# A scan, two quantized feed-forward layers and an attention block on one core: scaled third q, ternary rounding on ACT, norms on DVE, a butterfly on POOL, order planned by phase

## The chip, the cores and the metric

The kernel runs on one core of a Trainium2 chip. The time is the device time of one execution in microseconds (us); the figure of the kernel before is the median of three runs. PE is TensorE (PEld its weight loads), DVE is VectorE, ACT is ScalarE, POOL is GpSimd, SP is the queue that issues the DMAs.

## The reference

Two layers are added onto x, which has 128 sequences of 32 time steps and 256 features:

```python
x = x + L0_ffn(L0_cond(q0=cond, p0=cond, drive=x, coupling, bias), w_gate, w_up, w_down)
x = x + L1_ffn(L1_cond(x, emb=cond, ...), w_gate, w_up, w_down)

# L0_cond: 32 Runge-Kutta steps of coupled oscillators, each of four derivatives
dq = q - q ** 3 / 3.0 - p + drive + tanh(q) @ coupling.T + bias
dp = EPSILON * (q + ALPHA - BETA * p)        # after each step q and p are clipped to +-20
# L0_ffn: silu(gate) * up, inputs and weights rounded in blocks of 32 with a shared exponent
# L1_cond: rms norm, scale and shift from cond; q, k, v; per head, with 16 features,
q = rms_norm(q, g_q); k = rms_norm(k, g_k)   # then softmax(q k^T / 4) v, and o + o @ W_out
# L1_ffn: a Hadamard transform of the input ahead of each product, 8 bit rounding of it,
q = clip(round(w / mean(abs(w))), -1, 1) * mean(abs(w))   # ternary weights; silu(gate) * up
```

## The kernel before, in words

All work is one list of items. `Work.add` notes for each its engine, a cost in us, the buffers that it reads and writes, and a rank (its place in the program). Some 30 pools of tiles serve the buffers (`slim` 128x256, `mid` 128x512, `wide` 128x1024, `tiny` 128x32; PSUM banks `ps_stage`, `ps_sum`, `ps_turn`, `ps_gu` in phase one, four `ps_one` and two double `ps_two` in phase two). `Work.run` is a list scheduler: it places the items on five engines in the order in which they can start, by their costs, gaps between engines (`TAIL`, `HOP`, `WITHIN`) and free tiles. `Work.order` runs it 40 times forth and back over all items, taking the ends of one pass as the priorities of the next, and keeps the order that ends first. The engines then issue in that order, each its own queue, so an instruction whose input is late holds all that are behind it on its engine. `emit` (L1345) writes all items of phase one (rank below 100) before those of phase two. `keep_warm` puts products of zeros where the plan has gaps on PE (L1354).

Phase one has the scan and the first feed-forward layer. `step` (L577 on) is one scan step over 128 rows x 256 features. For each of the four derivatives a PSUM bank `ps[i]` gathers a linear part written by DVE (`nest`, one scalar_tensor_tensor, L552), the drive d times a scaled identity (`plus`, L587), tanh times the coupling matrix (`slope`, L594 and L601), and earlier slopes times a scaled identity. The cubes are a Square on ACT (L595) times q on POOL (L608). Sums w and z for the end of the step are kept in PSUM by more nests; at its end a DVE operation adds and clips q (L645) and another clips z, the scaled p (L653). `ffn0(t, q)` takes each step's result through the first layer: block maxima and scales on DVE (L688, L666, L678, L671), products with POOL (L914, L956, L964), clipping (L888), transposes by DMA (L434), gate and up on PE (L929), Silu (L937), down (L976), and at last the rms norm of the sum and its transposed copy into `xnT` (L1017), which all of phase two reads. Weights are prepared meanwhile: `mx_weight` for the first layer, and `ternary_weight` for the second, whose loads wait for scan step 24. That one takes the mean magnitude with Abs on ACT (L763), and then per half of a matrix compares on DVE with -0.5 of the mean (L791) and with 0.5 of it (L796).

Phase two, `tokens(g)`, takes 32 tiles of 128 tokens each. Products with `w_qkv` give q and k (L1125, bank `pqk`) and v (L1132, bank `pv`, half of it used). ACT squares q and k (L1142), DVE sums each head (L1143), and `rsqrt` finds the reciprocal root: an affine step on POOL (L1088), a first guess from the bits on DVE (L1091), ten small operations on POOL (L1099 to L1109). DVE multiplies q and k by it (L1148, L1155), POOL multiplies q by the gains (L1160), DVE transposes (L1167, L1169), PE makes small products per head (L1177), softmax runs over DVE and ACT (L1192, L1196, L1199), PE multiplies by v (L1207), and after the output product (L1230) the tokens are rounded to 8 bits (`quantum`, L1071 to L1079). Gate and up (L1263), Silu (L1271) and their product (L1278) follow. Then come three butterfly stages over 1024 columns, two instructions each (L1294), on POOL, DVE, POOL in the first 29 tiles and on DVE in the last three; a transpose (L526), a product with a 128-wide Hadamard matrix (L1305), the rounding (L1313, L1317), the down product (L1328) and the sum (L1335).

Of the kernel before, what the change touches and what calls it, by code (L numbers as in the profile page):

```python
# [13 lines left out]
I32 = mybir.dt.int32  # L14
AF = mybir.ActivationFunctionType
# [22 lines left out]
RSQRT = 8.0 / 3.0  # L38
# [61 lines left out]
class Work:  # L100
# [82 lines left out]
    def run(self, forth):  # L183
# [11 lines left out]
        self.issued, self.last, self.gone = [], dict.fromkeys(ready), set()  # L195
        for item in self.items:
            item.open = len(item.after if forth else item.before)
            item.ready = 0.0
            for b in item.bufs:
                b.left, b.end = 0, 0.0  # L200
                if b.slots and not b.fixed:
                    b.slot = None
                for s in b.slots:
                    s.free = 0.0
        pools = {}
        for item in sorted(self.items, key=lambda i: i.prio):
# [5 lines left out]
        for item in self.items:  # L212
            if not item.open:
                ready[item.engine].append(item)
        done = []
        while len(done) < len(self.items):
# [20 lines left out]
            idle = item.engine == PE and t > now[PE] + 0.05  # L237
# [20 lines left out]
            for i in item.before if forth else item.after:  # L258
                i.ready = max(i.ready, item.end + (self.gap(item, i) if forth else self.gap(i, item)))
                i.open -= 1  # L260
                if not i.open:
                    ready[i.engine].append(i)
        return done

    def order(self):

        for item in self.items:
            for a in item.after:
                a.before.append(item)
            for b in item.bufs:  # L270
                b.fixed = b.slot is not None
            item.prio = item.rank
        best = math.inf
        for n in range(self.ROUNDS):
            self.strict = n > 0
            done = self.run(True)
            end = max(item.end for item in done)
            if end < best:
                best, chosen = end, done
                places = [(b, b.slot) for item in done for b in item.bufs]  # L280
                times = [(item, item.start, item.end) for item in done]
                ends = [(b, b.end) for item in done for b in item.bufs]
            for item in self.items:
                item.prio = -item.end
            self.strict = True
            self.run(False)
            for item in self.items:
                item.prio = -item.end
        for b, slot in places:
            b.slot = slot  # L290
        for b, end in ends:
            b.end = end
        for item, start, end in times:
            item.start, item.end = start, end
        self.keep_warm(chosen)
        return chosen
# [26 lines left out]
def kernel(  # L323
# [153 lines left out]

    P2, P3, END, LAST = rk4()
    S = -END[4]
    h = DT  # L480
    K = (1.0 + h / 2, 1.0 - h / 2 * P2[1], 1.0 - h * P3[1])
    EYES = (h / 2 / K[0], h / 2 / K[1], h / K[2], h / 6, LAST[3], -LAST[4] - h / 6)
    C_SCALES = (*EYES[:3], -h / 6)
    CUBES = tuple((c / 3.0) ** 0.5 for c in (h / 2, h / 2, h, h / 6))
# [94 lines left out]
    def step(t, q, p, d):  # L579
# [11 lines left out]
        def slope(i, qi):  # L591

            th, sq = Buf(slim), Buf(slim)
            add(ACT, 0.32, lambda: nc.scalar.activation(th.ap, qi.ap, AF.Tanh), [qi], [th], rank=rank, table="silu")  # L594
            add(ACT, 0.31, lambda: nc.scalar.activation(sq.ap, qi.ap, AF.Square, scale=CUBES[i]), [qi], [sq], rank=rank)  # L595

            def mm():
                for c in range(NC):
                    for m in range(NC):
                        sl = slice(m * P, (m + 1) * P)  # L600
                        nc.tensor.matmul(  # L601
                            ps[i].ap[:, sl], lhsT=coup[i][:, c, sl], rhs=two(th.ap)[:, c, :],
                            start=False, stop=(c == NC - 1 and m == NC - 1),
                        )
# [23 lines left out]
        plus(2, 2, d)  # L628
        nest(w2, w, LAST[1] / LAST[2], q2, rank)
        nest(z, z, END[1] / END[2], q2, rank)  # L630
        nest(q3, ps[1], K[1], cube, rank, SUB)
        plus(2, 2, q3)
# [10 lines left out]
        add(  # L643
            DVE, 0.335,
            lambda: nc.vector._custom_dve(  # L645
                TENSOR_ADD_SAT, out=qn.ap, in0=ps[3].ap, in1=cube.ap, s0=CLAMP, s1=-CLAMP
            ),
            [ps[3], cube], [qn], rank=rank,
        )
        edge = ALPHA / BETA  # L650
        add(
            DVE, 0.335,
            lambda: nc.vector.tensor_scalar(  # L653
                z.ap, z.ap, (-CLAMP - edge) / S, (CLAMP - edge) / S, ALU.min, ALU.max
            ),
            [], [z], rank=rank,
        )
# [96 lines left out]
    def ternary_weight(w, dst, b_dst, n, rank, after):  # L754
        mag, lim = Buf(tiny), Buf(tiny)
# [29 lines left out]
        add(DVE, 0.1, lambda: ts(lim.ap[:, 0:1], ws, 0.5, None, MULT), [], fills=[lim], rank=rank, after=[own])  # L785
        add(DVE, 0.1, lambda: ts(lim.ap[:, 1:2], ws, -0.5, None, MULT), [], fills=[lim], rank=rank, after=[own])

        for part, raw in enumerate(raws):
            low, wq = Buf(wide), Buf(wide_bf)
            add(  # L790
                DVE, 0.65, lambda raw=raw, low=low: ts(low.ap, raw.ap, lim.ap[:, 1:2], None, ALU.is_lt),  # L791
                [raw, lim], [low], rank=rank, port=True,
            )
            add(
                DVE, 1.2,
                lambda raw=raw, low=low, wq=wq: stt(wq.ap, raw.ap, lim.ap[:, 0:1], low.ap, ALU.is_gt, SUB),  # L796
                [raw, lim, low], [wq], rank=rank, port=True,
            )
            turn_weight(wq, dst, b_dst, part, rows, rank)
# [94 lines left out]
    def ffn0(t, q):  # L894
# [101 lines left out]
        add(POOL, 0.72, rsqrt, [], [ms], rank=rank)  # L996
# [52 lines left out]
    for b_c, c_mat in zip(b_coup[:KPADS], coup):  # L1049
        k_pad = c_mat.rearrange("p c n -> p (c n)").rearrange("p (r a d) -> p r a d", a=4, d=D_HEAD)  # L1050
        pads_ready.append(
            add(POOL, 0.6, lambda k_pad=k_pad: nc.gpsimd.memset(k_pad, 0.0), [], [b_c], rank=float(T))
# [31 lines left out]
    def rsqrt(v, y, scale, eps, rank):  # L1084

        t, u = Buf(tiny), Buf(tiny)
        tt, ts = nc.gpsimd.tensor_tensor, nc.gpsimd.tensor_scalar
        add(POOL, 0.24, lambda: ts(v.ap, v.ap, scale, eps, MULT, ADD), [], [v], rank=rank)  # L1088
        add(
            DVE, 0.12,  # L1090
            lambda: nc.vector.tensor_scalar(  # L1091
                y.ap.bitcast(I32), v.ap.bitcast(I32), -0.5, float(0x5F3759DF), MULT, ADD
            ),
            [v], [y], rank=rank,
        )

        def steps():

            tt(t.ap, y.ap, y.ap, MULT)  # L1099
            tt(t.ap, t.ap, v.ap, MULT)  # L1100
            ts(t.ap, t.ap, -0.5, 1.5, MULT, ADD)
            tt(y.ap, y.ap, t.ap, MULT)

            tt(t.ap, y.ap, y.ap, MULT)
            tt(t.ap, t.ap, v.ap, MULT)
            ts(u.ap, t.ap, 1.0, -10.0 / 3.0, MULT, ADD)
            tt(u.ap, u.ap, t.ap, MULT)
            ts(u.ap, u.ap, 1.0, 5.0, MULT, ADD)
            tt(y.ap, y.ap, u.ap, MULT)  # L1109

        add(POOL, 2.4, steps, [v], [t, u, y], rank=rank, port=True)

    def tokens(g):
# [26 lines left out]
        sq_sum, rstd = Buf(tiny), Buf(tiny)  # L1140
        add(ACT, 0.26, lambda: nc.scalar.copy(v_pad.ap[:, :, :D_HEAD], heads(pv.ap[:, :N])), [pv], [v_pad], rank=rank)
        add(ACT, 0.477, lambda: nc.scalar.activation(sq.ap, pqk.ap, AF.Square), [pqk], [sq], rank=rank)  # L1142
        add(DVE, 0.6, lambda: nc.vector.tensor_reduce(sq_sum.ap, heads(sq.ap), AX.X, ADD), [sq], [sq_sum], rank=rank)  # L1143

        rsqrt(sq_sum, rstd, 1.0 / D_HEAD, EPS_RMS, rank)
# [38 lines left out]
        for k in range(0, PAIRS, PAIRS // 2):  # L1184
            add(
                PE, 0.55, lambda k=k: logits(range(k, k + PAIRS // 2)), [qT, kT], fills=[pl], rank=rank,
# [25 lines left out]
        for k in range(0, HEADS, HEADS // 2):  # L1212
            add(
                PE, 0.63, lambda k=k: attend(range(k, k + HEADS // 2)), [exT, v_pad], fills=[po], rank=rank,
# [70 lines left out]
        for s, engine in enumerate((POOL, DVE, POOL) if g < NT - 3 else (DVE, DVE, DVE)):  # L1285
            dst = Buf(wide)
            for e, op in enumerate((ADD, SUB)):
# [8 lines left out]
                add(engine, 0.6 if engine == DVE else 1.228, butterfly, [src], fills=[dst], rank=rank, port=True)  # L1296
# [120 lines left out]
```

## Time and profile before

| what | value |
|---|---|
| median of three runs (range) | 867.91 us (867.62 to 868.57) |
| the profiled execution, its span | 868.0 us, 866.2 us |
| busy: PE, PEld, DVE | 795.1 us (92%), 598.6 us (69%), 732.2 us (85%) |
| busy: ACT, POOL | 494.0 us (57%), 615.9 us (71%) |
| mean clock granted to TensorE | 0.986 |
| last scan state starts (L645) | 398.0 us |
| first product of phase two (L1125), last sum (L1335) | 431.3 us, 862.9 us |

Busy time is the time in which an engine executes. Matmuls are pipelined and their ends are modelled, so PE shown as busy isn't PE at its peak. A group of instructions has its line, engine, operation, tiles, shapes and count, then busy us and mean ns of one, then the engine's idle time just before them and what ended it. A wait is put down to the instruction that came last.

### The profile page before, as it was taken

The numbers are of one execution on the slowest core, as the hardware profiler recorded it, in microseconds if no ns is written. First come the engines' busy times: TensorE is split into PE (matmuls) and PEld (weight loads), VectorE is DVE, ScalarE is ACT, GpSimd is POOL, SyncE is SP. The second block draws the span as 40 slices with busy tenths as digits, with TensorE's granted clock in tenths as the row PEclk, the third lists the DMA queues.
The fourth block names the chain that finished last, engine by engine and source line by source line (L and its number), as shares of the span: only waits on it lengthen the run. The fifth ranks groups of instructions, "written<-read, shape, count | busy, mean of one in ns | idle before, by whom it ended". The sixth has DMA issues, their size and how long they took to land. (4 is left out here: it accounts for less than half of the span.)

```text
span 866.2 us, 26286 instructions
## 1 busy us (share of the span) xinstructions
PE 795.1 (92%) x10506; PEld 598.6 (69%) x10506; DVE 732.2 (85%) x1863; ACT 494.0 (57%) x1009; POOL 615.9 (71%) x955
## 2 busy tenths in 40 slices
PE   7789999999999999997789999999999999899986
PEld 4566778877788788775456667666667676576765
DVE  6889989999989999998677887778878788887694
ACT  3233465655466665754335667666767555776755
POOL 5698898888768888899574776656685676676320
PEclk9999999999999999999799999999999999999999
DMA  7222232313122242435500113221221221221334
GB/s 241 84 38 53 59 82 59 74 49 83 35 65 68 70 134 56 92 67 110 117 2 15 27 39 65 49 49 32 52 50 48 56 48 42 48 43 46 60 68 86
DMA packets 128891, 55.53 MB, mean 64 GB/s; under 512 B 102144, under 2 KB 127616, under 8 KB 128768
## 3 DMA queue, kind: packets, MB, share of 16 engines
q1 hardware_dynamic: 128768, 53.85, 26.9%
q8 instruction: 82, 1.34, 0.6%
q14 instruction: 41, 0.34, 0.1%
HBM read 21.32 MB, written 8.39 MB: 34 GB/s over the span
## 5 line engine op out<-in xcount | busy, mean ns | idle before, releaser
L1294 POOL TENSOR_TENSOR wide<-wide 128x512 f32<-128x512 f32 x116 | 149.1, 1306 | 68.7 <-DVE wide L1278 33.6
L601 PEld LDWEIGHTS ps_stage<-slim,coup 128*128 128x128 f32 x1024 | 129.3, 192 | 18.1 <-ACT slim L594 10.6
L601 PE MATMUL ps_stage<-slim,coup 128*128 128x128 f32 x1024 | 139.4, 279 | 0.6 <-ACT slim L594 0.3
L608 POOL TENSOR_TENSOR slim<-slim,slim 128x256 f32<-128x256 f32 x96 | 72.4, 755 | 27.7 <-ACT slim L595 23.0
L587 PE MATMUL ps_stage<-slim,eye 128*128 128x256 f32 x256 | 76.6, 392 | 8.1 <-DVE slim L552 7.8
L587 PE MATMUL ps_stage<-drives,eye 128*128 128x256 f32 x256 | 79.2, 392 | 3.3 <-DVE ps_stage L552 2.0
L956 POOL TENSOR_TENSOR mid<-mid,tiny 128x512 f32<-128x512 f32 x64 | 66.2, 1047 | 3.7 <-DVE tiny L678 3.2
L964 POOL TENSOR_TENSOR wide_bf<-mid,tiny 128x512 bf16<-128x512 fp8e4 x64 | 66.5, 1050 | 1.4 <-DVE mid L888 1.1
L594 ACT ACTIVATE slim<-slim 128x256 f32<-128x256 f32 x96 | 39.3, 409 | 47.4 <-DVE slim L552 44.6
L1305 PE MATMUL ps_two<-had_ffn,wide 128*128 128x128 f32 x512 | 63.3, 278 | 1.3 <-DVE wide L1278 1.2
L595 ACT ACTIVATE slim<-slim 128x256 f32<-128x256 f32 x96 | 39.2, 408 | 43.1 <-DVE slim L552 43.0
L1305 PEld LDWEIGHTS ps_two<-had_ffn,wide 128*128 128x128 f32 x512 | 59.9, 192 | 5.4 <-ACT wide L1300 1.9
L1125 PE MATMUL ps_one<-w_qkv_sb,xnT 128*128 128x512 f32 x128 | 60.7, 599 | 0.5 <-DVE mid L1196 0.2
L1313 ACT ACTIVATE wide<-ps_two,magic,tiny 128x1024 f32<-128x1024 f32 x32 | 38.5, 1203 | 39.5 <-DVE tiny L1079 28.0
L587 PEld LDWEIGHTS ps_stage<-slim,eye 128*128 128x128 f32 x256 | 42.0, 190 | 24.0 <-DVE slim L552 16.1
L1294 DVE TENSOR_TENSOR wide<-wide 128x512 f32<-128x512 f32 x76 | 53.3, 727 | 5.9 <-POOL wide L1294 5.9
L1278 DVE SCALAR_TENSOR_TENSOR wide<-ps_two,tiny,mid 128x512 f32<-128x512 f32 x64 | 46.4, 737 | 12.0 <-ACT mid L1271 11.3
L1207 PEld LDWEIGHTS ps_one<-v_pad,mid 32*32 32x32 f32 x4096 | 42.2, 106 | 20.8 <-issue 15.4
L1271 ACT ACTIVATE mid<-ps_two,tiny 128x512 f32<-128x512 f32 x64 | 43.0, 686 | 21.9 <-PE ps_two L1263 21.6
L1207 PE MATMUL ps_one<-v_pad,mid 32*32 32x17 f32 x4096 | 48.0, 181 | 4.5 <-issue 3.0
L587 PEld LDWEIGHTS ps_stage<-drives,eye 128*128 128x128 f32 x256 | 40.3, 193 | 12.3 <-DVE ps_stage L552 7.7
L1263 PEld LDWEIGHTS <-slim_bf 128*128 128x128 bf16 x256 | 24.0, 97 | 34.3 <-issue 8.3
(169 smaller groups left out, 2188.7 us busy)
## 6 DMA issues: line engine op xcount, KB each, us to landing
x_step<-in_x_dram SPq DMA_DIRECT2D x32, 128.0 KB, 2.1
x_add<-in_x_dram SPq DMA_DIRECT2D x32, 128.0 KB, 2.1
x_dram<-slim SPq DMA_DIRECT2D x32, 128.0 KB, 1.9
slim<-x_dram SPq DMA_DIRECT2D x32, 128.0 KB, 2.6
out_dram<-slim SPq DMA_DIRECT2D x32, 128.0 KB, 1.7
raws<-in_L_ffn_w_gate_dram SPq DMA_DIRECT2D x4, 512.0 KB, 4.8
raws<-in_L_ffn_w_up_dram SPq DMA_DIRECT2D x4, 512.0 KB, 6.3
raws<-in_L_ffn_w_down_dram SPq DMA_DIRECT2D x4, 512.0 KB, 4.0
```

Source lines behind the costliest of these rows:

```text
L587: PE, cost, lambda: nc.tensor.matmul(ps[i].ap, lhsT=eyes[eye], rhs=src.ap, start=False, stop=False),
L594: add(ACT, 0.32, lambda: nc.scalar.activation(th.ap, qi.ap, AF.Tanh), [qi], [th], rank=rank, table="silu")
L601: nc.tensor.matmul(ps[i].ap[:, sl], lhsT=coup[i][:, c, sl], rhs=two(th.ap)[:, c, :], start=False, stop=(c == NC - 1 and m == NC - 1),)
L608: POOL, 0.685, lambda: nc.gpsimd.tensor_tensor(sq.ap, sq.ap, qi.ap, MULT),
L956: lambda it=it, ks=ks: nc.gpsimd.tensor_tensor(blocks(it.ap), blocks(it.ap), spread(binv.ap[:, ks], BLOCK), MULT),
L964: lambda b8=b8, ks=ks, sl=sl: nc.gpsimd.tensor_tensor(blocks(bq.ap[:, sl]), blocks(b8.ap), spread(bscl.ap[:, ks], BLOCK), MULT),
L1125: nc.tensor.matmul(pqk.ap, lhsT=xnT_flat[:, c, tok], rhs=w_qkv_sb[:, c, : 2 * N], start=(c == 0), stop=(c == NC - 1),)
L1207: nc.tensor.matmul(by_v(po.ap)[row, hd, :], lhsT=by_head(exT.ap)[row, hd, :], rhs=v_pad.ap[row, hd, :], start=True, stop=True,)
L1271: lambda pgu=pgu, act=act: nc.scalar.activation(act.ap, pgu.ap[:, :HALF], AF.Silu, scale=sgu.ap[:, 0:1]),
L1278: lambda pgu=pgu, act=act, sl=sl: stt(it.ap[:, sl], pgu.ap[:, HALF:], sgu.ap[:, 1:2], act.ap, MULT, MULT),
L1294: eng.tensor_tensor(dv[:, :, e, :], sv[:, :, 0, :], sv[:, :, 1, :], op)
L1305: nc.tensor.matmul(pfh.ap[:, sl], lhsT=iT.ap[:, sl], rhs=had_ffn, start=True, stop=True)
```

## The change

- In a scan step the third q is kept scaled by S3, so that m4 can be added to z and clipped in one operation (`add_sat`), in place of a nest and a clip. The third tanh takes the inverse scale.
- The drive's share in the step's end is added by DVE into w (a nest), in place of a product on PE into ps[3].
- The ternary rounding is done on ACT: Identity with a large constant added, then Sign after taking it off.
- The reciprocal norms of q and k: sums, guess and a cubic polynomial on DVE, ten instructions in one item, with small tiles alternately in SBUF and in the unused half of `pv`.
- The middle butterfly goes from DVE to POOL for tiles below 27; the last five tiles have DVE, DVE, POOL.
- The two phases are ordered one after the other, each with its own 40 rounds; some costs are new (memset 1.0, norm on POOL 0.86, small products 0.48 and 0.57, butterfly on POOL 1.25).

```diff
     def order(self):
-        best = math.inf
-        for n in range(self.ROUNDS):
-            self.strict = n > 0
-            done = self.run(True)
...
+        chosen = []
+        for second in (False, True):
+            items = [item for item in self.items if (item.rank >= self.SECOND) == second]
+            best = math.inf
+            for n in range(self.ROUNDS):
+                self.strict = n > 0
+                done = self.run(items, True, chosen)
...
+                for back in (True, False):
+                    for item in items:
+                        item.prio = -item.end
+                    if back:
+                        self.strict = True
+                        self.run(items, False, ())
...
+            chosen += order
         self.keep_warm(chosen)
...
     def step(t, q, p, d):
         plus(2, 2, d)
+        nest(w, d, h / 6 / LAST[1], w, rank)
         nest(w2, w, LAST[1] / LAST[2], q2, rank)
         nest(z, z, END[1] / END[2], q2, rank)
-        nest(q3, ps[1], K[1], cube, rank, SUB)
-        plus(2, 2, q3)
+        nest(q3, ps[1], K[1] * S3, cube, rank)
+        plus(2, 6, q3)
...
-        plus(3, 3, d)
         plus(3, 4, q3)
-        nest(z, z, END[2] / END[3], q3, rank)
-        nest(m4, ps[2], -K[2], cube, rank)
+        nest(z, z, END[2] / S, q3, rank)
+        nest(m4, ps[2], -K[2], cube, rank, SUB)
         plus(3, 5, m4)
         cube = slope(3, m4)
-        nest(z, z, -END[3] / END[4], m4, rank)
-        add(DVE, 0.335, ... TENSOR_ADD_SAT, out=qn.ap, in0=ps[3].ap, in1=cube.ap ...)
-        add(DVE, 0.335, ... tensor_scalar(z.ap, z.ap, ..., ALU.min, ALU.max))
+        add_sat(z, z, m4, (CLAMP - edge) / S, (-CLAMP - edge) / S)
+        add_sat(qn, ps[3], cube, -CLAMP, CLAMP)
...
     def ternary_weight(w, dst, b_dst, n, rank, after):
-            add(DVE, 0.65, ... ts(low.ap, raw.ap, lim.ap[:, 1:2], None, ALU.is_lt) ...)
-            add(DVE, 1.2, ... stt(wq.ap, raw.ap, lim.ap[:, 0:1], low.ap, ALU.is_gt, SUB) ...)
+            add(ACT, 1.04, ... activation(y.ap, raw.ap, AF.Identity, bias=magic, scale=inv.ap[:, 0:1]) ...)
+            add(ACT, 1.04, ... activation(wq.ap, y.ap, AF.Sign, bias=neg_magic) ...)
...
+    def norms(sq, y, place, scale, eps, rank):
+            v, g, u = (place.ap[:, N + k * n : N + (k + 1) * n] for k in range(3))
+            nc.vector.tensor_reduce(v, heads(sq.ap), AX.X, ADD)
+            ts(x.ap, v, scale, eps, MULT, ADD)
+            ts(g.bitcast(I32), x.ap.bitcast(I32), -0.5, float(0x5F3759DF), MULT, ADD)
+            nc.vector.tensor_tensor(t.ap, g, x.ap, MULT)
+            nc.vector.tensor_tensor(u, g, t.ap, MULT)
+            ts(e.ap, u, -1.0, None, ADD)
+            stt(u, u, POLY[0] - 1.0, e.ap, ADD, MULT)
+            stt(u, u, POLY[1], e.ap, ADD, MULT)
+            stt(t.ap, u, POLY[2], e.ap, ADD, MULT)
+            stt(y.ap, t.ap, POLY[3], g, ADD, MULT)
+        add(DVE, 1.55, steps, [sq], [x, e, t, y], fills=[place], rank=rank)
...
-        for s, engine in enumerate((POOL, DVE, POOL) if g < NT - 3 else (DVE, DVE, DVE)):
+        for s, engine in enumerate((POOL, POOL, POOL) if g < NT - 5 else (DVE, DVE, POOL)):
```

More of the change, by code (lines that the diff above doesn't have):

```diff
@@ L37 @@
 EPS_QUANT = 1e-5
-RSQRT = 8.0 / 3.0
+RSQRT = 3.64945348
 PE, DVE, ACT, POOL, SP = "PE", "DVE", "ACT", "POOL", "SP"
@@ L181, in gap, with run @@
         return a.tail + self.TAIL[a.engine] + self.HOP[b.engine]
-    def run(self, forth):
+    def run(self, items, forth, before):
         ready = {e: [] for e in (PE, DVE, ACT, POOL, SP)}
@@ L194, in run @@
         port, table = 0.0, None
-        self.issued, self.last, self.gone = [], dict.fromkeys(ready), set()
-        for item in self.items:
-            item.open = len(item.after if forth else item.before)
+        self.issued, self.last, self.gone = [], dict.fromkeys(ready), set(before)
+        for item in items:
+            item.open = 0
             item.ready = 0.0
+            for a in item.after if forth else item.before:
+                if a in self.gone:
+                    item.ready = max(item.ready, a.end + self.gap(a, item))
+                elif (a.rank < self.SECOND) == (item.rank < self.SECOND):
+                    item.open += 1
             for b in item.bufs:
@@ L204, in run @@
                     s.free = 0.0
+        if forth:
+            for item in before:
+                now[item.engine] = max(now[item.engine], item.end)
+                self.last[item.engine] = item
+                table = item.table or table
+                for b in item.bufs:
+                    for s in b.slots:
+                        s.free = 0.0
+            for item in before:
+                for b in item.bufs:
+                    if b.slots:
+                        s = b.slots[b.slot]
+                        s.free = max(s.free, item.end + item.tail + self.TAIL[item.engine] + 0.06)
         pools = {}
-        for item in sorted(self.items, key=lambda i: i.prio):
+        for item in sorted(items, key=lambda i: i.prio):
             for b in item.bufs:
@@ L211, in run @@
                 b.left += 1
-        for item in self.items:
+        for item in items:
             if not item.open:
@@ L215, in run @@
         done = []
-        while len(done) < len(self.items):
+        while len(done) < len(items):
             best = None
@@ L236, in run @@
             ready[item.engine].remove(item)
-            idle = item.engine == PE and t > now[PE] + 0.05
+            idle = item.engine == PE and t > now[PE] + 1.5 * self.COLD
             item.start, item.end = t, t + item.cost + (self.COLD if idle else 0.0)
@@ L258, in run @@
             for i in item.before if forth else item.after:
[L259 to L262, printed above, removed]
+                if (i.rank < self.SECOND) == (item.rank < self.SECOND):
+                    i.ready = max(i.ready, item.end + (self.gap(item, i) if forth else self.gap(i, item)))
+                    i.open -= 1
+                    if not i.open:
+                        ready[i.engine].append(i)
         return done
@@ L272, in order @@
             item.prio = item.rank
-        best = math.inf
-        for n in range(self.ROUNDS):
-            self.strict = n > 0
-            done = self.run(True)
[L277 to L294, printed above, removed]
+        chosen = []
[5 more added lines that the diff above has]
+                done = self.run(items, True, chosen)
+                end = max(item.end for item in done)
+                if end < best:
+                    best, order = end, done
+                    places = [(b, b.slot, b.end) for item in done for b in item.bufs]
+                    times = [(item, item.start, item.end) for item in done]
+                for back in (True, False):
+                    for item in items:
+                        item.prio = -item.end
+                    if back:
+                        self.strict = True
+                        self.run(items, False, ())
+            for b, slot, end in places:
+                b.slot, b.end = slot, end
+            for item, start, end in times:
+                item.start, item.end = start, end
+            chosen += order
         self.keep_warm(chosen)
@@ L479 @@
     S = -END[4]
+    S3 = END[3] / S
     h = DT
     K = (1.0 + h / 2, 1.0 - h / 2 * P2[1], 1.0 - h * P3[1])
-    EYES = (h / 2 / K[0], h / 2 / K[1], h / K[2], h / 6, LAST[3], -LAST[4] - h / 6)
+    EYES = (h / 2 / K[0], h / 2 / K[1], h / K[2], h / 6, LAST[3] / S3, -LAST[4] - h / 6, h / K[2] / S3)
     C_SCALES = (*EYES[:3], -h / 6)
-    CUBES = tuple((c / 3.0) ** 0.5 for c in (h / 2, h / 2, h, h / 6))
+    CUBES = tuple((c / 3.0) ** 0.5 for c in (h / 2, -S3 * h / 2, -h / S3**3, h / 6))
     eyes = []
@@ L593, in slope @@
             th, sq = Buf(slim), Buf(slim)
-            add(ACT, 0.32, lambda: nc.scalar.activation(th.ap, qi.ap, AF.Tanh), [qi], [th], rank=rank, table="silu")
+            add(ACT, 0.32, lambda: nc.scalar.activation(th.ap, qi.ap, AF.Tanh, scale=1.0 / S3 if i == 2 else 1.0), [qi], [th], rank=rank, table="silu")
             add(ACT, 0.31, lambda: nc.scalar.activation(sq.ap, qi.ap, AF.Square, scale=CUBES[i]), [qi], [sq], rank=rank)
@@ L635, in step, with add_sat @@
         add(ACT, 0.27, lambda: nc.scalar.mul(ps[3].ap, w2.ap, LAST[2]), [w2], [ps[3]], rank=rank)
-        plus(3, 3, d)
         plus(3, 4, q3)
-        nest(z, z, END[2] / END[3], q3, rank)
-        nest(m4, ps[2], -K[2], cube, rank)
+        nest(z, z, END[2] / S, q3, rank)
+        nest(m4, ps[2], -K[2], cube, rank, SUB)
         plus(3, 5, m4)
         cube = slope(3, m4)
-        nest(z, z, -END[3] / END[4], m4, rank)
[L643 to L649, printed above, removed]
-        edge = ALPHA / BETA
[L651 to L657, printed above, removed]
+        edge = ALPHA / BETA
+        def add_sat(dst, in0, in1, low, high):
+            add(
+                DVE, 0.335,
+                lambda: nc.vector._custom_dve(TENSOR_ADD_SAT, out=dst.ap, in0=in0.ap, in1=in1.ap, s0=high, s1=low),
+                [b for b in (in0, in1) if b is not dst], [dst], rank=rank,
+            )
+        add_sat(z, z, m4, (CLAMP - edge) / S, (-CLAMP - edge) / S)
+        add_sat(qn, ps[3], cube, -CLAMP, CLAMP)
         return qn, z
@@ L754, in ternary_weight @@
     def ternary_weight(w, dst, b_dst, n, rank, after):
-        mag, lim = Buf(tiny), Buf(tiny)
+        mag, inv = Buf(tiny), Buf(tiny)
         raws = []
@@ L784, in ternary_weight @@
         own = b_ws.writers[-1]
-        add(DVE, 0.1, lambda: ts(lim.ap[:, 0:1], ws, 0.5, None, MULT), [], fills=[lim], rank=rank, after=[own])
-        add(DVE, 0.1, lambda: ts(lim.ap[:, 1:2], ws, -0.5, None, MULT), [], fills=[lim], rank=rank, after=[own])
+        add(DVE, 0.17, lambda: nc.vector.reciprocal(inv.ap[:, 0:1], ws), [], [inv], rank=rank, after=[own])
         for part, raw in enumerate(raws):
-            low, wq = Buf(wide), Buf(wide_bf)
+            y, wq = Buf(wide), Buf(wide_bf)
             add(
-                DVE, 0.65, lambda raw=raw, low=low: ts(low.ap, raw.ap, lim.ap[:, 1:2], None, ALU.is_lt),
-                [raw, lim], [low], rank=rank, port=True,
-            )
-            add(
-                DVE, 1.2,
-                lambda raw=raw, low=low, wq=wq: stt(wq.ap, raw.ap, lim.ap[:, 0:1], low.ap, ALU.is_gt, SUB),
-                [raw, lim, low], [wq], rank=rank, port=True,
+                ACT, 1.04,
+                lambda raw=raw, y=y: nc.scalar.activation(
+                    y.ap, raw.ap, AF.Identity, bias=magic, scale=inv.ap[:, 0:1]
+                ),
+                [raw, inv], [y], rank=rank,
+            )
+            add(
+                ACT, 1.04, lambda y=y, wq=wq: nc.scalar.activation(wq.ap, y.ap, AF.Sign, bias=neg_magic),
+                [y], [wq], rank=rank,
             )
@@ L994, in rsqrt @@
             nc.gpsimd.tensor_tensor(m1(), m1(), neg_half, ALU.pow)
-        add(POOL, 0.72, rsqrt, [], [ms], rank=rank)
+        add(POOL, 0.86, rsqrt, [], [ms], rank=rank)
         if t < T - LATE:
@@ L1051 @@
         pads_ready.append(
-            add(POOL, 0.6, lambda k_pad=k_pad: nc.gpsimd.memset(k_pad, 0.0), [], [b_c], rank=float(T))
+            add(POOL, 1.0, lambda k_pad=k_pad: nc.gpsimd.memset(k_pad, 0.0), [], [b_c], rank=float(T))
         )
@@ L1082, in quantum @@
         return am, sc
[L1084 to L1095, printed above, removed]
-        def steps():
[L1099 to L1111, printed above, removed]
+    POLY = (-1.14571778, 1.36854794, -1.82472059, RSQRT)
+    def norms(sq, y, place, scale, eps, rank):
+        n = 2 * HEADS
+        x, e, t = Buf(tiny), Buf(tiny), Buf(tiny)
+        ts = nc.vector.tensor_scalar
+        def steps():
+            v, g, u = (place.ap[:, N + k * n : N + (k + 1) * n] for k in range(3))
[10 more added lines that the diff above has]
+        add(DVE, 1.55, steps, [sq], [x, e, t, y], fills=[place], rank=rank)
     def tokens(g):
@@ L1139, in tokens @@
         v_pad, sq, qn, k_pad = Buf(v_pads), Buf(mid), Buf(slim), Buf(k_pads)
-        sq_sum, rstd = Buf(tiny), Buf(tiny)
+        rstd = Buf(tiny)
         add(ACT, 0.26, lambda: nc.scalar.copy(v_pad.ap[:, :, :D_HEAD], heads(pv.ap[:, :N])), [pv], [v_pad], rank=rank)
         add(ACT, 0.477, lambda: nc.scalar.activation(sq.ap, pqk.ap, AF.Square), [pqk], [sq], rank=rank)
-        add(DVE, 0.6, lambda: nc.vector.tensor_reduce(sq_sum.ap, heads(sq.ap), AX.X, ADD), [sq], [sq_sum], rank=rank)
-        rsqrt(sq_sum, rstd, 1.0 / D_HEAD, EPS_RMS, rank)
+        norms(sq, rstd, pv, 1.0 / D_HEAD, EPS_RMS, rank)
         add(
@@ L1185, in tokens @@
             add(
-                PE, 0.55, lambda k=k: logits(range(k, k + PAIRS // 2)), [qT, kT], fills=[pl], rank=rank,
+                PE, 0.48, lambda k=k: logits(range(k, k + PAIRS // 2)), [qT, kT], fills=[pl], rank=rank,
                 records=BT * PAIRS, small=True,
@@ L1213, in tokens @@
             add(
-                PE, 0.63, lambda k=k: attend(range(k, k + HEADS // 2)), [exT, v_pad], fills=[po], rank=rank,
+                PE, 0.57, lambda k=k: attend(range(k, k + HEADS // 2)), [exT, v_pad], fills=[po], rank=rank,
                 records=BT * HEADS, small=True,
@@ L1294, in butterfly @@
                     eng.tensor_tensor(dv[:, :, e, :], sv[:, :, 0, :], sv[:, :, 1, :], op)
-                add(engine, 0.6 if engine == DVE else 1.228, butterfly, [src], fills=[dst], rank=rank, port=True)
+                add(engine, 0.6 if engine == DVE else 1.25, butterfly, [src], fills=[dst], rank=rank, port=True)
             src = dst
```

## The prediction

> **What bounds the kernel now.** I read the busy time by stage first, cutting at the points where the work changes: the scan starts, all engines run, the last scan step is written (398.0), the first token tile begins (431).
>
> ```profile
> 100.00:340.00 240.00, 237.17 (x1583) 190.13 (x1582) 224.15 (x646) 139.92 (x402) 202.24 (x275) 1.00 0.30 71
> 340.00:398.00 58.00, 55.74 (x371) 43.84 (x370) 56.03 (x155) 33.90 (x96) 53.87 (x71) 1.00 0.34 75
> 398.00:431.00 33.00, 22.26 (x122) 14.61 (x122) 25.81 (x56) 15.02 (x38) 24.15 (x31) 0.79 0.56 124
> 450.00:823.00 373.00, 346.64 (x7486) 254.42 (x7479) 299.06 (x724) 240.75 (x345) 242.34 (x452) 0.99 0.21 45
> ```
>
> The columns after the length are busy us of PE, weight loads, DVE, ACT and POOL. In 100:340 PE is idle 2.8 us of 240: phase one is bound by TensorE, with DVE (224) close behind. Then DVE passes PE (56.0 of 58). In the 33 us between the last scan step and the first token tile nothing is full: a chain of latencies. In phase two PE is 93% busy by the modelled ends, DVE 80%, so no engine is full, and waits matter.
>
> Next, the groups of PE in 100:340, to turn that into a step of the scan.
>
> ```profile
> L601 PE MATMUL ps_stage<-slim,coup 128*128 128x128 f32 x677 | 91.4, 278 | 0.1
> L587 PE MATMUL ps_stage<-drives,eye 128*128 128x256 f32 x170 | 51.8, 386 | 0.2 <-DVE ps_stage L552 0.2
> ```
>
> A step makes 32 records of L601 (four stages, four products, two records each), so 677 are 21.2 steps, 11.3 us each. Per step that is PE 11.2, DVE 10.6, POOL 9.5, ACT 6.6 us. L587 on the drive makes 8 records a step, 386 ns each, but they overlap: the timeline shows what they occupy.
>
> ```profile
> 234.93 0.60 PE L587 MATMUL ps_stage<-drives,eye 128*128 128x256 f32 x2
> 235.36 0.59 PE L929 MATMUL ps_gu<-w0uT,slim_bf 128*128 128x512 bf16 x2
> ```
>
> One drive product (two records) holds PE for 235.36 - 234.93 = 0.43 us.
>
> Last, who DVE waits for in 431:866 (total us, times, longest).
>
> ```profile
> DVE slim L1148 <- POOL tiny L1109: 17.3, 18, 2.7
> DVE tiny L1143 <- ACT mid L1142: 15.8, 15, 4.1
> DVE wide L1278 <- ACT mid L1271: 11.3, 12, 1.8
> DVE coup L1155 <- POOL tiny L1109: 7.3, 7, 1.6
> DVE wide L1294 <- POOL wide L1294: 5.9, 6, 1.8
> DVE tiny L1091 <- POOL tiny L1088: 2.1, 6, 0.4
> ```
>
> Four of these six, 17.3 + 7.3 + 5.9 + 2.1 = 32.6 us, are waits for POOL.
>
> **What the Trainium skill says.** "VectorE: DVE Perf Modes", section "The DRAIN you can't avoid", says that a read after a write on the same engine needs a semaphore, while an instruction that isn't held may start before the one ahead of it has ended. The trace agrees: L671, which does not need L678, starts 0.10 us after it; L1079, which reads L1078's result, starts 0.18 after it.
>
> ```profile
> 407.37 0.18 DVE L678 TENSOR_SCALAR tiny<-ps_sum 128x32 int32<-128x32 int32 x1
> 407.47 0.18 DVE L671 TENSOR_SCALAR tiny<-ps_sum 128x32 int32<-128x32 int32 x1
> ...
> 510.87 0.15 DVE L1078 TENSOR_SCALAR tiny<-tiny 128x1 f32<-128x1 f32 x1
> 511.05 0.16 DVE L1079 RECIPROCAL tiny<-tiny 128x1 f32<-128x1 f32 x1
> ```
>
> "SBUF — State Buffer", section "Who interferes with whom": DVE and GpSimd share a pair of ports; a tensor_scalar between SBUF tiles can take the pair, one with PSUM on a side does not. The trace fits: L1091, SBUF to SBUF, has a median of 180 ns and a longest of 1262, about one butterfly of POOL (1306).
>
> ```profile
> L1091 DVE TENSOR_SCALAR tiny<-tiny x32: 115/180/1262, 434.9 to 785.3; 128x32 int32<-128x32 int32 x32
> ```
>
> "ScalarE: Activation LUTs", section "Table sets: the hidden batching unit", names identity and abs among the functions that every set holds, and does not name sign. The compiled order shows no table load at the Sign instructions, so I charge none. A load is 1283 ns on that page and in this trace.
>
> **The change, part by part.** The profiled execution took 868.0 us (span 866.2, 1.8 around it); the median is 867.91, so a sum from 868.0 needs no correction.
>
> *Scaled third q and drive on DVE (every scan step).* PE loses one product of drive and eye, 0.43 us. DVE gains one nest (d into w), but adding m4 into z and clipping z become one add-and-saturate, 0.42 each, so its count of 256-wide instructions stays at 15: nothing added. The third tanh gets a scale and keeps its form (L594, 409 ns). PE falls from 11.2 to 10.8 us per step; DVE stays at 10.6 and is next. So the step can shrink by 0.43 at most, and I take 0.3, because a wait in either engine now costs. From 100 to 398 there are 26 steps: 8 us. Before 100 the weights bound and I take none. Ends: 0 (DVE already sets the step) and 11. One eye more, 0.5 us of POOL at the start, is beside DMA.
>
> *Ternary rounding on ACT.* Six halves each lose a compare (0.75 us, L791) and a second pass (1.28, L796) on DVE, 12 us, and gain two activations on ACT. Nearest rows: L763, 1.05, and L1317, 1.15; so 2 x 1.1 x 6 = 13 us. On DVE only two passes of each kind lie before 398 (L791 at 346.3 and 389.2, L796 at 352.6 and 396.8), 4 us in a stretch where DVE is 97% busy. On ACT the compiled order puts four roundings near the last two steps, each in front of a tanh or a square that the scan waits for, up to 1.1 us each: net gain 2, ends -3 and +4. In the tail the last L796 (1.28 at 428.21) stands between L1012 and L1014 of the last tile, and it goes: 1 us. The other eight roundings lie there on ACT, 15.0 busy of 33; they hide in its 18 idle us, and up to 2 us show if one stands ahead of an xnT copy. Transposing DMAs on SP stay as many. Lim's two small operations against one reciprocal: nothing.
>
> *Norms on DVE.* POOL loses eleven 128x32 instructions a tile, 89 us in all with 2.5 us of gaps a tile. DVE loses L1091 (0.2) and gains nine small instructions, each reading the one before. Price: 0.10 apart if not held, 0.18 to 0.21 held; the compiled order shows a wait at each, so 0.19 x 9 = 1.7, and the reduction must end first, 0.1 more. That is +1.6 a tile, +51 us on DVE; ends +22 and +60. During it DVE serves nobody else: silu products (L1278), maxima (L1071) and softmax queue behind it. The scheduler books 1.55 us for all ten; I get 0.68 + 1.7 = 2.4. The third bank of pv is held longer, but four banks serve the uses of a 13.5 us tile.
>
> *Middle butterfly on POOL.* 76 DVE butterflies become 20: 56 x 0.60 (two take 1.27, so 0.60 apart) = 34 us off DVE; ends 34 and 41 (mean 727 with its waits). POOL gains 56 x 1.31 = 73, less than the 89 it loses: -16. The last five tiles keep two stages on DVE and put the third on an idle POOL: latency +1.4 a tile, less DVE queue; zero, +-1.
>
> *Phase two together.* DVE: 51 - 34 = +17 us of work, -32.6 of waits for POOL: -16 if DVE alone set the pace. PE's work is unchanged and its idle time in 450:823 is only 26 us, so I take half: -8. Ends: -24 and +20. Six table loads fewer (30 to 24) are 8 us of an ACT that has room: inside that half.
>
> *Order by phase, new costs.* No trace prices an order. It moves nearly every instruction; I take 0, ends -8 and +8.
>
> Sum: -8 -2 -1 -8 = -19, so 868 - 19 = 849.
>
> **The rivals.** *A: the waits go whole.* With norms and all three butterflies uninterrupted, the 32.6 us go and the 17 of work fit into DVE's idle time (74 of 373); phase one gives its 11: 868 - 11 - 3 - 25 = 829. For it: all four waits are removed at their source. Against: PE would have almost no idle time left. *B: phase two gives nothing.* The norm's block replaces the waits: 868 - 11 = 857. For it: at +17 us DVE has PE's load. *C: slower.* One mechanism: the norms' ten instructions outlast their booking by 0.9 us, and DVE's queue is in order, so silu products and maxima come late for PE, which has to follow the booked order. 32 x 0.9 = 29 us on the path, less 11 from phase one, gives 886 if no wait is saved; with a third of the 32.6 saved, 875. It decides from the point where the steps are over 0.19 us apart and PE's idle share in phase two grows instead of shrinking. *D: no change*, gains and C cancel: 868.
>
> **How the numbers follow.** Forecast (840 to 856) 0.48; A (822 to 840) 0.22; B (856 to 866) 0.16; D 0.04; C (870 to 886) 0.10. The likeliest gives 849. The range 828 to 869 leaves out about 0.07 of A and the 0.10 of C. Faster by over 0.2% (about what a measurement of this kernel can tell from no change): 0.86; within: 0.04; slower: 0.10.
>
> **What would show it.** Right: a scan step near 11.0 us in the middle with PE still full; the scan's last state before 390; no DVE wait on POOL before qn's product; the nine steps 0.18 to 0.21 apart; first token tile near 420; phase two near 427. Wrong: a step of 11.3 with DVE full; L1278 and L1071's successors late, PE idle above 40 us in phase two; ACT roundings ahead of a tanh in the chain.

## The result and the profile after

The changed kernel takes 897.25 us (median of four, 896.61 to 901.75), the kernel before 867.76 beside it: ratio 1.035 (95% interval 1.032 to 1.039). The forecast was 849.0, range 828 to 869, so it was wrong, and on the wrong side. The profiled execution is the slowest of the four; it has a span of 900.0 us.

The busy time by stage of the changed kernel comes first (length, then busy us of PE, weight loads, DVE, ACT, POOL, with counts), cut where the kernel before was cut.

```profile
100.00:340.00 240.00, 236.49 (x1576) 185.46 (x1576) 230.60 (x659) 143.47 (x410) 210.54 (x286) 1.00 0.33 74
340.00:398.00 58.00, 54.54 (x367) 42.07 (x365) 55.88 (x160) 43.85 (x109) 53.02 (x72) 1.00 0.45 103
398.00:431.00 33.00, 22.16 (x93) 12.36 (x93) 15.02 (x45) 14.95 (x32) 13.67 (x20) 0.84 0.30 64
450.00:823.00 373.00, 330.06 (x6699) 240.17 (x6700) 284.44 (x841) 215.30 (x313) 213.45 (x184) 0.96 0.19 41
```

The scan looks alike, PE full and DVE a little fuller. But in 450:823 every engine does less than before: PE 330 us against 347, DVE 284 against 299, ACT 215 against 241, POOL 213 against 242. DVE and POOL have exchanged work, but PE's products are the same. No engine is fuller than before, so no single engine's load explains this; the question is who waits for whom.

The points between the stages say the same. The last scan state and the first product of phase two (the last two numbers before the semicolon are the first and the last start of the group):

```profile
L672 DVE CUSTOM_DVE_ANT_0 states<-ps_stage,slim x32: 411/424/426, 31.5 to 388.9; 128x256 f32<-128x256 f32 x32
L1146 PE MATMUL ps_one<-w_qkv_sb,xnT x128: 592/592/1061, 420.8 to 815.2; 128*128 128x512 f32 x128
```

The last scan state is written at 388.9 us (before 398.0) and phase two begins at 420.8 (before 431.3): 10 us won. Phase two then lasts 479 us instead of 435: 44 us lost.

Who waits for whom in phase two, 421:900 (engine, tile and line, who it waited for, total us, times, longest):

```profile
PE ps_one L1153 <- DVE tiny L1130: 26.8, 16, 3.2
...
ACT v_pad L1162 <- PE ps_one L1153: 38.0, 14, 7.4
...
ACT v_pad L1162 <- DVE tiny L1130: 20.2, 8, 3.4
...
DVE ps_one L1121 <- PE ps_one L1153: 7.3, 7, 2.2
...
POOL slim L1179 <- DVE slim L1167: 88.1, 19, 15.6
```

L1153 is the product that makes v, L1162 its copy to SBUF, L1121 to L1130 the ten norm instructions, L1167 the first reader of the norms. By the reference, v has nothing to do with the norms of q and k. Yet the product waits for the norms' last step, and the copy too. All waits of DVE for POOL from the prediction's table are gone, as they should be.

Listed by the line of the product, weight loads included, it is 27 waits and 44.7 us:

```profile
L1153 PE MATMUL ps_one<-w_qkv_sb,xnT x128: 379/379/795, 426.2 to 821.4; 128*128 128x256 f32 x128
...
  DVE tiny L1130: 44.7, 27
```

The same group in the kernel before, with its two longest waits:

```profile
L1132 PE MATMUL ps_one<-w_qkv_sb,xnT x128: 379/379/793, 436.5 to 803.2; 128*128 128x256 f32 x128
...
  ACT v_pad L1141: 2.9, 4
  DVE coup L1155: 2.0, 5
```

(PE and weight-load records of one instruction both count there, so 44.7 is more than PE's idle time.) The timeline shows one instance on both engines, of the third tile:

```profile
432.54 0.68 DVE L1121 TENSOR_REDUCE ps_one<-mid 128x32 f32<-128x512 f32 x1
433.26 0.19 DVE L1122 TENSOR_SCALAR tiny<-ps_one 128x32 f32<-128x32 f32 x1
433.48 0.20 DVE L1123 TENSOR_SCALAR ps_one<-tiny 128x32 int32<-128x32 int32 x1
...
434.86 0.19 DVE L1129 SCALAR_TENSOR_TENSOR tiny<-ps_one,tiny 128x32 f32<-128x32 f32 x1
435.08 0.19 DVE L1130 SCALAR_TENSOR_TENSOR tiny<-tiny,ps_one 128x32 f32<-128x32 f32 x1
...
435.42 2.76 PE L1153 MATMUL ps_one<-w_qkv_sb,xnT 128*128 128x256 f32 x8 [2.29 <-DVE tiny L1130]
...
436.56 0.37 ACT L1162 COPY v_pad<-ps_one 128x256 f32<-128x256 f32 x1 [4.57 <-PE ps_one L1153]
```

The square brackets give the idle time ahead and who ended it. PE stood 2.29 us with v's product at the head of its queue, all its later work behind it, while DVE did norms; ACT stood 4.57 us behind the copy. The block of ten takes 432.54 to 435.27, 2.73 us, against 1.55 booked (the cost that the planner is given).

Why: v's product writes columns 0 to 255 of the buffer `pv`, the norms keep v, g and u in columns 256 to 351. The columns don't overlap, but both write into one PSUM tile, and in the trace the one that is issued later waits for the one issued earlier. In 20 token tiles the norms come first, and in 17 of them the product starts within 0.2 us of their end. In the other 12 the product comes first; in 10 of them the norms start within 0.2 us of its end, and the copy of v within 0.1 us of the norms' end. The planner knows nothing of it: `place` is named under `fills`, which makes no order among writers.

### The profile page after: what moved, and what is told of

It reads as the page before. It is cut to its first block, busy times and chain, and to the rows that moved or that the text cites. A ratio compares the mean times of both kernels' runs of the same rounds, so it can differ in the third digit from the quotient of the medians.

```text
span 900.0 us, 26130 instructions
## 1 busy us (share of the span) xinstructions
PE 802.5 (89%) x10451; PEld 595.9 (66%) x10451; DVE 734.4 (82%) x2048; ACT 499.0 (55%) x1015; POOL 590.3 (66%) x660
## 4 chain that ended last, share of the span: by engine, by line
PE 30%; DVE 22%; ACT 6%; issue 4%; DMA 3%; POOL 2%; DVEq 0%; ACTq 0%; SPq 0%; POOLq 0%
PE ps_one L1146 3%; PE ps_two L1324 3%; PE ps_one L1153 3%; PE ps_two L1282 3%; PE ps_two L551 2%; DVE ps_one L1121 2%; PE ps_one L1249 2%; PE ps_one L1226 2%; PE ps_one L1196 2%; DVE tiny L1092 2%; DMA wide_bf<-wide_bf 2%; PE ps_stage L626 2%; PE ps_stage L612 2%; ACT wide L1332 2%; DVE wide L1313 1%
## 5 line engine op out<-in xcount | busy, mean ns | idle before, releaser
L1313 POOL TENSOR_TENSOR wide<-wide 128x512 f32<-128x512 f32 x172 | 216.0, 1285 | 99.6 <-DVE wide L1297 61.2
L1179 POOL TENSOR_TENSOR slim<-slim,g_prod 128x256 f32<-128x256 f32 x32 | 23.4, 730 | 123.0 <-DVE slim L1167 88.1
L633 POOL TENSOR_TENSOR slim<-slim,slim 128x256 f32<-128x256 f32 x96 | 72.6, 757 | 24.3 <-ACT slim L620 18.6
L612 PE MATMUL ps_stage<-slim,eye 128*128 128x256 f32 x256 | 80.7, 399 | 3.9 <-DVE slim L577 2.9
L1324 PE MATMUL ps_two<-had_ffn,wide 128*128 128x128 f32 x512 | 65.3, 283 | 4.8 <-ACT wide L1319 4.3
L1324 PEld LDWEIGHTS ps_two<-had_ffn,wide 128*128 128x128 f32 x512 | 62.3, 197 | 8.3 <-ACT wide L1319 5.7
L1153 PE MATMUL ps_one<-w_qkv_sb,xnT 128*128 128x256 f32 x128 | 38.1, 427 | 29.7 <-DVE tiny L1130 26.8
L620 ACT ACTIVATE slim<-slim 128x256 f32<-128x256 f32 x96 | 39.1, 407 | 43.9 <-DVE slim L577 41.8
L612 PE MATMUL ps_stage<-drives,eye 128*128 128x256 f32 x192 | 60.7, 400 | 2.8 <-DVE ps_stage L577 2.1
L612 PEld LDWEIGHTS ps_stage<-slim,eye 128*128 128x128 f32 x256 | 40.0, 192 | 24.2 <-DVE slim L577 18.1
L1092 DVE TENSOR_REDUCE tiny<-ps_two 128x1 f32<-128x1024 f32 x32 | 38.8, 1212 | 20.9 <-PE ps_two L1324 20.7
L1162 ACT COPY v_pad<-ps_one 128x256 f32<-128x256 f32 x32 | 11.9, 371 | 72.8 <-PE ps_one L1153 38.0
```

The source lines that it names most:

```text
L612: PE, cost, lambda: nc.tensor.matmul(ps[i].ap, lhsT=eyes[eye], rhs=src.ap, start=False, stop=False),
L1092: lambda: nc.vector.tensor_reduce(am.ap[:, 0:1], src.ap[:, :n], AX.X, ALU.max, apply_absolute_value=True),
L1153: nc.tensor.matmul(pv.ap[:, :N], lhsT=xnT_flat[:, c, tok], rhs=w_qkv_sb[:, c, 2 * N :], start=(c == 0), stop=(c == NC - 1),)
L1313: eng.tensor_tensor(dv[:, :, e, :], sv[:, :, 0, :], sv[:, :, 1, :], op)
L1324: nc.tensor.matmul(pfh.ap[:, sl], lhsT=iT.ap[:, sl], rhs=had_ffn, start=True, stop=True)
```

## The experiments

Theory T: norms and v share a tile, and the plan does not book the wait. Rival R: the block outlasts its booking (case C of the prediction). Rival S: the order by phase, or POOL with every butterfly, is to blame. All times are medians with the kernel before beside them.

**The first four: undo, move away, tell, book.**

norm_pool puts back the head sums on DVE and the root on POOL (the constant RSQRT too), nothing else.

```diff
-        norms(sq, rstd, pv, 1.0 / D_HEAD, EPS_RMS, rank)
+        add(DVE, 0.6, ... tensor_reduce(sq_sum.ap, heads(sq.ap), AX.X, ADD) ...)
+        rsqrt(sq_sum, rstd, 1.0 / D_HEAD, EPS_RMS, rank)
```

> Changed kernel with the norms undone (head sums on DVE, reciprocal root on POOL as before), all else kept. T and R: 845 to 862, phase two near 430. S: 885 or more.

843.5 us, ratio 0.972 (0.968 to 0.975), just under the range of T and R. The norms carry the whole loss; S is out, and the rest of the change is worth 25 us.

told names `pv` among the writes, which makes the planner put the norms behind v's product and copy. (Its first pass of phase two also takes tiles by rank, and a pass that finds no free tile is skipped. The first of these is in all kernels named told and in no other, and no run has it alone.)

```diff
-        add(DVE, 1.55, steps, [sq], [x, e, t, y], fills=[place], rank=rank)
+        add(DVE, 1.55, steps, [sq], [x, e, t, y, place], rank=rank)
```

> Changed kernel in which the scheduler is told that the norms write v's bank (so it places them after v's product and its copy), and the first planning pass of phase two takes tiles in order of rank; same instructions. T: PE's wait for the last norm step goes, 848 to 872. R and S: 890 or more.

866.8 us, ratio 0.997 (0.996 to 0.998), 30 less than the change, with the same instructions in another order. The waits at v's product (L1154 here), by that line:

```profile
L1154 PE MATMUL ps_one<-w_qkv_sb,xnT x128: 379/379/483, 422.9 to 798.9; 128*128 128x256 f32 x128
...
  DVE tiny L1131: 3.8, 4
```

44.7 us became 3.8. The time is in T's range; R alone would have left 890 or more.

booked_270 leaves the planner ignorant and books 2.7 for the block.

```diff
-        add(DVE, 1.55, steps, [sq], [x, e, t, y], fills=[place], rank=rank)
+        add(DVE, 2.7, steps, [sq], [x, e, t, y], fills=[place], rank=rank)
```

> Changed kernel with the norm item booked at 2.7 us instead of 1.55; the shared bank stays. T: v's product still waits for the norms, 885 to 905. R: the order fits the real length, 855 to 870. S: 890 to 900.

877.1 us, ratio 1.009 (1.007 to 1.011): below T's range and above R's. The wait stays (63.7 us, 35 times at L1153), so T is not mended. It is even longer than the 44.7 of the slower changed kernel: what a wait costs depends on what stands behind it, and the sum of waits doesn't rank the kernels. Whether 20 us came from the right length or from a luckier order this run can't say.

norm_sbuf gives v, g and u three SBUF tiles of their own.

```diff
+        three = [Buf(tiny) for _ in range(3)]
-            v, g, u = (place.ap[:, N + k * n : N + (k + 1) * n] for k in range(3))
+            v, g, u = (b.ap for b in three)
-        add(DVE, 1.55, steps, [sq], [x, e, t, y], fills=[place], rank=rank)
+        add(DVE, 1.55, steps, [sq], [x, e, t, y, *three], rank=rank)
```

> Changed kernel with v, g and u of the norms in three SBUF tiles of their own instead of the free half of v's PSUM bank. Theory T (norms and v's product share one PSUM tile, so one waits for the other, and the plan does not book that): PE no longer waits for the last norm step, phase two falls from 479 to about 430 us, time 845 to 862. Rival R (the norm block lasts 2.78 us where 1.55 is booked): still 890 or more. Rival S (order by phase or the third POOL butterfly): still 890 or more.

907.4 us, ratio 1.044 (1.041 to 1.048): T's number missed by 45. No wait for the norms is left at v's product, but something else came. Its timeline of one block, with POOL's butterflies (L1314) beside it:

```profile
478.95 7.38 POOL L1314 TENSOR_TENSOR wide<-wide 128x512 f32<-128x512 f32 x6
...
480.68 0.81 DVE L1123 TENSOR_SCALAR tiny<-tiny 128x32 f32<-128x32 f32 x1
481.52 1.19 DVE L1124 TENSOR_SCALAR tiny<-tiny 128x32 int32<-128x32 int32 x1
482.75 1.20 DVE L1125 TENSOR_TENSOR tiny<-tiny,tiny 128x32 f32<-128x32 f32 x1
483.98 1.18 DVE L1126 TENSOR_TENSOR tiny<-tiny,tiny 128x32 f32<-128x32 f32 x1
485.19 1.18 DVE L1127 TENSOR_SCALAR tiny<-tiny 128x32 f32<-128x32 f32 x1
486.40 0.19 DVE L1128 SCALAR_TENSOR_TENSOR tiny<-tiny,tiny 128x32 f32<-128x32 f32 x1
```

Four steps that take 0.19 us alone take 1.2, one after another, and the one before them 0.81. POOL's six butterfly instructions take 7.38 us, 1.23 each, and each of the five steps ends within 0.05 us of the end of one of them. The Trainium skill, "SBUF — State Buffer", section "Who interferes with whom", says of the ports that DVE and GpSimd share that the pair is held for a whole instruction and the other engine blocks; this fits, five times in one block. Over all 32 blocks the mean is 3.9 us, where a block of the changed kernel takes 2.7, and PE now waits 24.3 us for silu products of DVE (L1298), 4.5 in the changed kernel. So the run does not tell T from R: it trades one wait for another.

**Do T and R add, and is it luck?** told_booked is told with 2.7 booked; after_165 is the changed kernel with 1.65 booked, which gives the plan no better information and makes another one.

> The kernel told, with the norm item booked at 2.7 us as well. If the two unbooked things (T: the shared bank; R: the length) add, 843 to 858, near the kernel with norms on POOL. If they are one and the same loss, no better than told: 862 to 872.

846.8 us, ratio 0.977 (0.975 to 0.979).

> Control for the luck of the plan: the changed kernel with the norm item booked at 1.65 instead of 1.55, which makes another order and mends neither thing. T and R: still slow, 880 to 905. If the loss is an unlucky order, anywhere, below 875 too.

881.2 us, ratio 1.015 (1.011 to 1.018). A change of 0.1 in one booking moves the time by 16 us, so single differences of that size prove nothing about a booking. Hence three more, and one that books the length in the variant without the shared tile:

> The kernel told with 1.65 booked in place of 1.55: another order, neither worse nor better informed. Plan luck alone moves it within 867 +- 10. T holds if it stays below 878, where the untold kernel with 1.65 took 881; T falls as the main cause if it takes 880 or more.

864.0 us, ratio 0.994 (0.992 to 0.995).

> The kernel told with 2.9 booked, a little over what the block takes. If the booking of the length is worth something beside the shared bank (R), 840 to 855 as with 2.7; if the 847 with 2.7 was a lucky order, 860 to 872.

852.3 us, ratio 0.981 (0.977 to 0.985).

> Changed kernel with 2.9 booked and the shared bank not told. If a right length is worth nothing while the bank is unbooked, 875 to 890, the same as with 1.65 and 2.7; if R works by itself, below 870.

901.4 us, ratio 1.035 (1.031 to 1.039), above both of its ranges.

> Kernel norm_sbuf (no shared bank) with the block booked at 3.4 us, about the sum of its steps in that run. R: the 907 of norm_sbuf came from a block of 3.6 booked at 1.55, so now 845 to 865. If blocking at the ports is a cost of its own, 880 to 910.

903.3 us, ratio 1.038 (1.034 to 1.041). R's range is missed, but R isn't refuted: in this order the steps are blocked more (their means run from 192 to 618 ns), and the 32 blocks took 2.65 to 7.60 us, 4.5 on average, so 3.4 was again too little. The planner can keep operations that need the shared ports apart (`port=True`, set for the butterflies); neither this run nor norm_sbuf sets it for the norms, so what that would give is open.

Together, in us; in brackets the length of phase two in the profiled execution. That is the better measure where an edit touches phase two alone, for in such kernels the first scan state starts anywhere from 28.8 to 32.7 us.

| booked | 1.55 | 1.65 | 2.7 | 2.9 |
|---|---|---|---|---|
| shared tile not told | 897.3 (479.2) | 881.2 (458.8) | 877.1 (457.5) | 901.4 (479.2) |
| told | 866.8 (448.0) | 864.0 (443.8) | 846.8 (427.5) | 852.3 (434.1) |

Told is faster in each column, by 17 to 49, on average 32; in phase two by 15 to 45, on average 30. The wait of v's product for the last norm step, by its line, is 44.7 to 63.7 us in the four kernels above and 0.3 to 3.8 in the four below. Without telling, a right length shows no gain (889.2 on average in the two left columns, 889.3 in the two right), but the pairs are 16 and 24 us apart, so a gain of that size could be hidden. With it, a right length is worth 16 (865.4 against 849.6), with pairs 3 and 6 apart. So T is the main cause, and R a second one that is seen only where T is mended. The other first pass of the told kernels doesn't tell the planner of that wait, but that it has a share in the 32 is not ruled out.

**The norms without the rest.** before_norms has the norms of the change, in `pv` at 1.55, in the kernel before.

> The kernel before with the norms alone changed (DVE, booked 1.55, three small tiles in v's bank). T and R: the norms carry the loss whatever the order and the butterflies, 895 to 925, with PE's v product waiting for the last norm step. If the loss needs the other edits, 860 to 880.

924.5 us, ratio 1.065 (1.062 to 1.068), with 50.6 us, 24 times, of v's product waiting for the last norm step. Phase two takes 481.4 us against 434.9 before, and it begins 7 us later too, for here both phases are planned together. The loss needs no other edit.

**What the other edits are worth**, each against norm_pool (843.5). np_mid_dve has the butterfly engines of before, np_joint the planner's `run` and `order` of before, np_drive_pe the drive's product on PE again, np_booked the true length of POOL's root.

```diff
-        for s, engine in enumerate((POOL, POOL, POOL) if g < NT - 5 else (DVE, DVE, POOL)):
+        for s, engine in enumerate((POOL, DVE, POOL) if g < NT - 3 else (DVE, DVE, DVE)):
...
-        nest(w, d, h / 6 / LAST[1], w, rank)
+        plus(3, 3, d)
...
-        add(POOL, 2.4, steps, [v], [t, u, y], rank=rank, port=True)
+        add(POOL, 3.25, steps, [v], [t, u, y], rank=rank, port=True)
```

> Kernel norm_pool with the butterfly engines of before (POOL, DVE, POOL; DVE in the last three tiles). If the middle butterfly on POOL helps beside norms on POOL, 848 to 860; if POOL with both norms and all butterflies is too full, 830 to 842; neutral 842 to 847.

852.6 us, ratio 0.983 (0.980 to 0.985): 9 more. Of the profiled executions, 4.2 of that lie ahead of phase two, which this edit doesn't touch; phase two is 430.6 us there and 424.9 in norm_pool, so the move to POOL is worth about 6.

> Kernel norm_pool with both phases ordered together in 40 rounds, as before. If the order by phase is worth something, 848 to 862; if nothing, 840 to 847; if it costs, below 840.

853.2 us, ratio 0.983 (0.980 to 0.985): order by phase is worth 10. Phase two begins at 420.3 there, 416.9 in norm_pool, and lasts 430.1 us against 424.9.

> Kernel norm_pool with the drive's share of the step's end back on PE (one product more and one nest less in each scan step). The forecast's step: the middle of the scan is bound by PE, so 0.3 us a step comes back on 26 steps and the time is 848 to 855. If DVE sets the step instead, DVE is freed of 0.33 a step and the time is 832 to 843.

860.9 us, ratio 0.991 (0.988 to 0.993), 17 more and beyond its ranges. Only part of that is the scan: from first to last state 360.7 us against 356.0, 4.6 us. The stretch from the last state to phase two is 41.5 us there and 32.0 in norm_pool; I put that down to another plan and not to the product, but no run shows it.

> Kernel norm_pool with POOL's reciprocal root booked at what it takes (3.25 for the ten, 0.30 for the affine step, instead of 2.4 and 0.24). R in general form (an item that outlasts its booking costs time): 832 to 841. If only items on a full engine matter, 841 to 848.

844.3 us, ratio 0.971 (0.968 to 0.974): no gain in the total. In the profiled execution phase two is 421.2 us against 424.9, so the same kind of error in a booking costs at most a little here, with POOL 319 us busy of 425. These four differences are of the size of the plan's luck (16 us) too, so they are rough.

norm_pool is the fastest version; told_booked, with all of the change, comes within 4 us of it. So even told and booked, the norms on DVE gain nothing over those on POOL.

## Why the prediction was wrong, point by point

*The scan and the start of phase two: the sum right, in part by luck.* Forecast: last state before 390, first token tile near 420. Measured 388.9 and 420.8. The sum of two terms held: from the first to the last state 367.0 us became 357.4, -9.6, forecast -8 -2. The parts did not. The middle of the scan (the states between 100 and 340) fell from 11.29 to 11.15 us a step, 0.14 and not 0.3: 3 us over these 20 steps and not 6. The last five steps gave 6.7 us, where 0.3 a step and the 2 for the roundings make 3.5, with ACT at 43.9 busy of 58 and the scan unharmed by it. Nor is the 0.14 the drive's alone: with the drive's product back on PE a step takes 11.21, with the joint order 11.38, where norm_pool has 11.12. PE stayed full (236.5 of 240) with a product less in each step, and DVE filled from 224 to 231; why only a third of the 0.43 came isn't shown.

*Ternary rounding on ACT: right.* L811 takes 1236 ns, L817 1151, forecast 1.1 each. The stretch from the last state to phase two is 31.9 us, from 33.3: -1.4, forecast -1. No table load came with Sign.

*Norms: work nearly right, length an eighth short.* The nine steps start 0.225 to 0.233 apart (medians), just outside the forecast's 0.18 to 0.21; the block is 2.73 and not 2.4. DVE is busy 355.6 us in phase two against 340.9, +15, forecast +17.

*The step that failed* is the sentence "The third bank of pv is held longer, but four banks serve the uses of a 13.5 us tile". It took the norms' place in v's buffer as a matter of room. It is one of order: two engines write into one tile, so in 27 of the 32 token tiles v's product, or its copy, starts right at the end of that tile's norm block, with PE's or ACT's queue behind it. "Phase two together" (-8) then became +44. The working asked half of the right question: it named what queues behind the norms on DVE, and not who else touches the tile that they fill. With that told and the length booked the kernel takes 847 to 852, which is the forecast's 849, and phase two 427.5 and 434.1, forecast near 427. The sum of the other terms came out, but not each of them: the order by phase, put at 0, was worth about 10 beside norms on POOL, so the rest came to less than forecast.

*Order, taken as 0 with ends of 8:* too narrow. With one booking 0.1 higher the same instructions, in another order, moved by 16 us.

*Rival C* had the sign, 0.10 chance, and its sign in the profile: PE's idle time in 450:823 rose from 26 to 43 us, over the 40 that the forecast named; its range, 870 to 886, was still too low. Its mechanism, late DVE products because of a block that outlasts its booking, is not what made most of the loss: PE's waits for silu products in phase two are 4.5 us, and booking the length without telling the tile changed nothing on average. It is 16 us once the tile is told.

*Open.* A PSUM bank is one tile here, so whether the wait belongs to the tile or to the bank was not separated: no bank is free in phase two. And no run tells the planner that norms in SBUF need the shared ports.

## What to carry to other kernels

Free columns of a tile that another engine writes are room, not independence: look in the trace for waits between the two before counting on them, and if they stand, tell the planner. Ask of each added instruction not only who waits for its result but who else writes or reads the tile that it writes. And when the order comes from a list scheduler, repeat an experiment at a few harmless bookings before believing a difference of 1 or 2%.

## What the runs showed of the hardware

A chain of 128x32 DVE instructions, each reading the one before and alternating between PSUM and SBUF, starts one every 0.225 to 0.233 us, where a 128x1 pair took 0.18. The same chain within SBUF, beside butterflies on POOL, was blocked at step after step: five in a row took 0.81 to 1.20 us where 0.19 is their length alone, while the chain with PSUM on one side of each step (longest step 0.20 us) never was. And TensorE's granted clock was 0.962 in the changed kernel and 0.953 in norm_sbuf, against 0.984 and 0.989 in told and told_booked. PE stands still for 68 and 76 us of phase two in the first two, 47 and 28 in the others. That the one makes the other is not shown; norm_pool, with 32 us, had 0.980.
